# Running a graph's input stage beside the preceding graph's list stage in a graph-network kernel

## The chip, the cores and the metric

The kernel runs on one core of a Trainium2 chip. The metric is the device time of one execution in microseconds (us). Before the change three executions took 4073.46, 4090.68 and 4098.83 us; the median, 4090.68 us, is the number that the change is compared with. One further execution was profiled (4057.96 us, a profiled span of 4056.2 us); all lines of profile below come from it.

The engines have these names here: PE is the matrix engine (PEld its weight loads), DVE the vector engine, ACT the scalar engine, POOL the GpSimd engine, SP the engine that only issues DMA transfers. Each engine runs its own list of instructions in the order in which the program gives them, and waits at one that is not ready.

## The reference, cut to what matters

There are 16 graphs of 1024 nodes with 64 channels, and a weighted adjacency matrix per graph.

```python
x = _layernorm(x + _L0_gnn_ref(...))     # layer 0: messages = adj @ h; dh = tanh([h, messages] @ W1 + b1) @ W2 + b2
x = _layernorm(x + _L1_gnn_ref(...))     # layer 1, below

def _L1_gnn_ref(x, adj, mask, W1, b1, W2, b2):
    adj_d = _dilate_adj(adj, mask)                         # drops up to two neighbours of a node, by rank
    agg = _weighted_nanquantile_agg(x, adj_d > 0)          # per node and channel: sort the neighbours' values,
                                                           # weighted sum of the 0.25, 0.5, 0.75 quantiles
    out = x + agg
    return (relu(out @ W1 + b1) @ W2 + b2) * mask
```

The expensive part is that every node needs the values of its own neighbours sorted, channel by channel. Most nodes have few neighbours, a few (hubs) have very many.

## The kernel before

The kernel has two halves. The **front** of a graph reads its adjacency matrix, computes layer 0, orders the nodes by degree and makes each node's list of neighbours. The **units** gather the neighbours' rows from a table in HBM (one indirect DMA, issued by POOL, for each place of a list and each 128 nodes) and sort them on DVE with a network of min and max operations. Graphs are handled in groups of four: the units of a group start when its four fronts are there. The hubs of all graphs come last; the largest ones (168 neighbours) are one long DVE sort at the end.

```python
FRONT_NS, UNITS_NS = 185e3, 360e3      # estimated DVE time of a group's fronts, and of its units
...
def bank(name):                        # PSUM: 4 single banks, and two double ones (bank2)
    return psum.tile([P, HALF], F32, tag="bank", name=name, bufs=4)
...
desc = cp.tile([P, NT, N], F16, name="s_desc")     # N - column, for each of the 8 row tiles, 0 on the diagonal
...
def front(pool, grp, b, infs, out_ids, made):      # pool has one buffer of each tag unless it says more
    x_sb = pool.tile([P, NT, C], F32, tag="x_sb", name="x_sb", bufs=2)
    SY.dma_start(x_sb, x[b].rearrange("(t p) c -> p t c", p=P))
    score = pool.tile([P, NT, N], F16, tag="score", name="score")
    node = pool.tile([P, N], F32, tag="node", name="node")
    m = counts[:, b, :NT]
    for h in range(2):                             # ---- input stage: 8 row tiles
        pn = bank("pn")
        for k in range(NT // 2):
            t = h * (NT // 2) + k
            a_sb = pool.tile([P, N], F32, tag="a_sb", name="a_sb", bufs=3)
            SY.dma_start(a_sb, adj[b, t * P:(t + 1) * P, :])
            V.scalar_tensor_tensor(score[:, t, :], a_sb, 0.0, desc[:, t, :], op0=ALU.is_gt, op1=ALU.mult)
            ... # PE transposes a_sb through two banks, ACT copies them to aT
            junk = pool.tile([P, N], BF16, tag="junk", name="junk", bufs=2)
            A.activation(junk, score[:, t, :], AF.Sign, accum_out=m[:, t:t + 1])   # degree
            ... # PE: pn += x_sb and aT (messages)
            yield
        A.copy(node[:, h * HALF:(h + 1) * HALF], pn)
    ...                                            # ---- list stage: PE writes the keys of all nodes
    for t in range(NT):                            # ACT: the place of every node in the order by degree
        junk = pool.tile([P, N], BF16, tag="junk", name="junk", bufs=2)
        A.activation(junk, keys, AF.Sign, bias=nkey[:, t:t + 1], accum_out=place[:, t:t + 1])
    yield
    V.tensor_tensor(pre, pd.rearrange("p (t c) -> p t c", c=C), x_sb, op=ALU.add)
    yield
    ... # DVE: perm (8 operations, a yield after every second); PE: pi, and ps = perm x score, 8 x 16 matmuls
    yield from layernorm(pool, pre, rows[:, :, :C])
    ...
    for s in range(1, NT):
        V.max(mine_l[:, 1:9], slots[s])            # the first eight neighbours; two slots need a second round
        if s + 2 < NT:
            permuted(s + 2)                        # next 16 matmuls into a double bank
        yield
    ... # the neighbours to drop; POOL writes them to the table (removes); index and own for the units
    made.append((index, own))
    yield

def finish(pool, xs, u, mask, out_index):          # end of a unit: PE pu, ACT uT, PE ph, ACT hid, PE py in one go
    ...
    for _ in range(4):
        yield
    ... # DVE: residual, layernorm; POOL writes the rows out
```

A generator gives its turn away at each `yield`. The loop that builds the program takes a step of the fronts or of the units by comparing the estimated DVE time spent in each:

```python
def fronts(pool):
    for gi in range(groups):
        ...
        for g in range(G):
            yield from front(pool, grp, gi * G + g, infs, out_ids, made)   # one graph after the other
        ready[gi] = (infs, out_ids, made)
        yield
...
with tc.manual_schedule(engines={E.DVE, E.Activation, E.PE, E.Pool}):      # program order; SP is ordered by the framework
    ...
            behind = spent_f[0] / FRONT_NS - 1 <= spent_u[0] / UNITS_NS
            if behind or metered(work, spent_u) is False:                  # False: the next group isn't ready
                if metered(ahead, spent_f) == "over":
                    break
```

Of the kernel before, what the change touches and what calls it, by code (L numbers as in the profile page):

```python
# [11 lines left out]
F32 = mybir.dt.float32  # L12
F16 = mybir.dt.float16
# [13 lines left out]
C = 64  # L27
# [176 lines left out]
FRONT_NS, UNITS_NS = 185e3, 360e3  # L204
LW = 18

# [18 lines left out]
def sparse(ctx, tc, x, adj, nodemask, w1a, b1a, w2a, b2a, w1b, b1b, w2b, b2b, consts, out,  # L225
# [10 lines left out]
    def bank(name):  # L236
        return psum.tile([P, HALF], F32, tag="bank", name=name, bufs=4)
# [17 lines left out]
    desc = cp.tile([P, NT, N], F16, name="s_desc")  # L255
    GP.iota(desc, pattern=[[0, NT], [-1, N]], base=N, channel_multiplier=0,
# [34 lines left out]
    with tc.tile_pool(name="s_init", bufs=1) as pool:  # L291
        sel_f = pool.tile([2 * NT, NT * P], F32, name="sel_f")
        SY.dma_start(sel_f, consts[0:2 * NT, slice(*_CONSTS["sel"])])
        V.tensor_copy(sel.rearrange("k t p -> k (t p)"), sel_f)
        off_diag = pool.tile([P, P], F16, name="off_diag")
        V.tensor_scalar(off_diag, ident, -1.0, 1.0, op0=ALU.mult, op1=ALU.add)
        for t in range(NT):
            here = slice(t * P, (t + 1) * P)
            V.tensor_tensor(desc[:, t, here], desc[:, t, here], off_diag, op=ALU.mult)
        mask_u8 = pool.tile([P, P], U8, name="mask_u8")  # L300
        SY.dma_start(mask_u8, nodemask.rearrange("b (t p) -> (b t) p", p=P))
        mask_f = pool.tile([P, P], F32, name="mask_f")
        V.tensor_copy(mask_f, mask_u8)
        pm = bank("pm")
        T.transpose(pm[:, :P], mask_f, ident)
        V.memset(info, 0.0)
        V.tensor_copy(info[:, :, :, 1], pm[:, :P].rearrange("p (b t) -> p b t", t=NT))
        for b in range(B):
            V.tensor_copy(info[:, b, :, 0], node_id)
            V.tensor_copy(counts[:, b, NT:], rev)  # L310
# [15 lines left out]
    hub_infos = [dram.tile([B * n, 8], F32, name=f"hub_infos{c}")  # L326
# [4 lines left out]
    def layernorm(pool, src, dst):  # L331

        K = src.shape[1]
        mean = pool.tile([P, K], F32, tag="ln_mean", name="ln_mean")
        V.tensor_reduce(mean, src, axis=AX.X, op=ALU.add)
        V.tensor_scalar(mean, mean, 1.0 / C, None, op0=ALU.mult)
        xm = pool.tile([P, K, C], F32, tag="ln_xm", name="ln_xm")
        V.tensor_tensor(xm, src, mean.unsqueeze(2).to_broadcast([P, K, C]), op=ALU.subtract)
        sq = pool.tile([P, K, C], F32, tag="ln_sq", name="ln_sq")
        A.activation(sq, xm, AF.Square)  # L340
        yield
        yield
        var = pool.tile([P, K], F32, tag="ln_var", name="ln_var")
        V.tensor_reduce(var, sq, axis=AX.X, op=ALU.add)
        V.tensor_scalar(var, var, 1.0 / C, EPS, op0=ALU.mult, op1=ALU.add)
        e = pool.tile([P, K], F32, tag="ln_e", name="ln_e")
        A.activation(e, var, AF.Sqrt)
        yield
        yield
        y = pool.tile([P, K], F32, tag="ln_y", name="ln_y")  # L350
        V.reciprocal(y, e)

        V.tensor_tensor(e, y, y, op=ALU.mult)
        V.tensor_tensor(e, e, var, op=ALU.mult)
        V.tensor_scalar(e, e, -0.5, 1.5, op0=ALU.mult, op1=ALU.add)
        V.tensor_tensor(y, y, e, op=ALU.mult)
        V.tensor_tensor(dst, xm, y.unsqueeze(2).to_broadcast([P, K, C]), op=ALU.mult)

    def front(pool, grp, b, infs, out_ids, made):

        g = b % G
        x_sb = pool.tile([P, NT, C], F32, tag="x_sb", name="x_sb", bufs=2)
        SY.dma_start(x_sb, x[b].rearrange("(t p) c -> p t c", p=P))
        score = pool.tile([P, NT, N], F16, tag="score", name="score")
        node = pool.tile([P, N], F32, tag="node", name="node")
        m = counts[:, b, :NT]
        for h in range(2):
            pn = bank("pn")  # L370
            for k in range(NT // 2):
                t = h * (NT // 2) + k
                a_sb = pool.tile([P, N], F32, tag="a_sb", name="a_sb", bufs=3)
                SY.dma_start(a_sb, adj[b, t * P:(t + 1) * P, :])
                V.scalar_tensor_tensor(score[:, t, :], a_sb, 0.0, desc[:, t, :],
                                       op0=ALU.is_gt, op1=ALU.mult)
                aT = pool.tile([P, NT, P], F32, tag="aT", name="aT", bufs=2)
                for hh in range(2):
                    pt = bank("pt")
                    for kk in range(NT // 2):  # L380
                        jt = hh * (NT // 2) + kk
                        T.transpose(pt[:, kk * P:(kk + 1) * P], a_sb[:, jt * P:(jt + 1) * P],  # L382
                                    ident)
                    A.copy(aT[:, hh * (NT // 2):(hh + 1) * (NT // 2), :]  # L384
                           .rearrange("p a b -> p (a b)"), pt)
                junk = pool.tile([P, N], BF16, tag="junk", name="junk", bufs=2)
                A.activation(junk, score[:, t, :], AF.Sign, accum_out=m[:, t:t + 1])  # L387
                cols = slice(k * P, (k + 1) * P)
                T.transpose(pn[:C, cols], x_sb[:, t, :], ident)
                for jt in range(NT):  # L390
                    T.matmul(pn[C:, cols], x_sb[:, jt, :], aT[:, jt, :],  # L391
                             start=(jt == 0), stop=(jt == NT - 1))
                yield
            A.copy(node[:, h * HALF:(h + 1) * HALF], pn)


# [10 lines left out]
        hid = pool.tile([C, N], F32, tag="hid", name="hid")  # L407
        for h in range(2):
            ph = bank("ph")
            T.matmul(ph[:C], w1a_sb, node[:, h * HALF:(h + 1) * HALF], start=True, stop=True)  # L410
            A.activation(hid[:, h * HALF:(h + 1) * HALF], ph[:C], AF.Tanh, bias=b1a_sb)
# [5 lines left out]
        place = pool.tile([P, NT], F32, tag="place", name="place", bufs=2)  # L417
        for t in range(NT):
            junk = pool.tile([P, N], BF16, tag="junk", name="junk", bufs=2)
            A.activation(junk, keys, AF.Sign, bias=nkey[:, t:t + 1],  # L420
                         accum_out=place[:, t:t + 1])
# [38 lines left out]
        V.memset(lists, 0.0)  # L460
        V.tensor_scalar(lists[:, :, 0], inf[:, 1:, 0], -1.0, float(N), op0=ALU.mult, op1=ALU.add)
# [50 lines left out]
        V.tensor_scalar(removes, gone, -1.0, float(N), op0=ALU.mult, op1=ALU.add)  # L512
# [15 lines left out]
        hinf = pool.tile([P, 8], F32, tag="hinf", name="hinf", bufs=2)  # L528
        V.memset(hinf[:, 6:7], float(b * ROWS + N))
        V.memset(hinf[:, 7:8], float(b * N))  # L530
        V.tensor_copy(hinf[:, 0:3], inf[:, 0, 0:3])
        V.tensor_copy(hinf[:, 3:4], own[:, 0:1])
        V.tensor_copy(hinf[:, 4:6], gone[:, 0, :])
        for c, (first_slot, n, _, _) in enumerate(CLASSES):
            SY.dma_start(hub_infos[c][b * n:(b + 1) * n, :], hinf[first_slot:first_slot + n, :])

        index = grp.tile([P, NT - 1, LW], I32, tag=f"index{g}", name="index", bufs=2)
        V.tensor_scalar(index, lists, -1.0, float(N + b * ROWS), op0=ALU.mult, op1=ALU.add)
# [91 lines left out]
    def finish(pool, xs, u, mask, out_index):  # L630
# [6 lines left out]
        A.copy(uT, pu[:C, :K * P])  # L637
        ph = bank("ph1")
        T.matmul(ph[:, :K * P], w1b_sb, uT, start=True, stop=True)  # L639
        hid = pool.tile([H1, K * P], F32, tag="hid1", name="hid1")  # L640
        A.activation(hid, ph[:, :K * P], AF.Relu, bias=b1b_sb)
        py = bank("py")
# [4 lines left out]
        for _ in range(4):  # L647
            yield
# [13 lines left out]
    def hub_lists(pool, c, tiles, src, xpool, xtag, xbufs):  # L662
# [3 lines left out]
        hinf = pool.tile([P, K, 8], F32, tag="uhinf", name="uhinf", bufs=4)  # L666
        out_index = pool.tile([P, K], I32, tag="hout", name="hout", bufs=4)
        X = xpool.tile([P, cap + 1, K, W], F32, tag=xtag, name="X", bufs=xbufs)
        for k, tl in enumerate(tiles):
# [11 lines left out]
            for q in range(2):  # L681
                V.scalar_tensor_tensor(ls, ls, hinf[:, k, 4 + q:5 + q], ls,
                                       op0=ALU.not_equal, op1=ALU.mult)
            ix = pool.tile([P, rounds * 8], I32, tag="hub_ix", name="hub_ix")
            V.tensor_scalar(ix, ls, -1.0, hinf[:, k, 6:7], op0=ALU.mult, op1=ALU.add)
            me = pool.tile([P, 1], I32, tag="hub_me", name="hub_me", bufs=2)
            V.scalar_tensor_tensor(me, hinf[:, k, 0:1], -float(N), hinf[:, k, 6:7],
                                   op0=ALU.add, op1=ALU.add)
            V.tensor_tensor(out_index[:, k:k + 1], hinf[:, k, 0:1], hinf[:, k, 7:8], op=ALU.add)
# [52 lines left out]

    def fronts(pool):
        for gi in range(groups):
            infs = grp.tile([P, G, NT, 4], F32, tag="infs", name="infs")
            out_ids = grp.tile([P, G, NT], I32, tag="out_ids", name="out_ids")
            made = []
            for g in range(G):
                yield from front(pool, grp, gi * G + g, infs, out_ids, made)
            ready[gi] = (infs, out_ids, made)  # L750
            yield
# [79 lines left out]
    with tc.manual_schedule(engines={E.DVE, E.Activation, E.PE, E.Pool}), ExitStack() as body:  # L831
# [532 lines left out]
```

## Time and profile before

| what | us |
|---|---|
| median of three executions | 4090.68 |
| profiled span | 4056.2 |
| first gather of group 0 issued | 385.23 |
| last front's `removes` written by POOL | 2605.0 |
| span after 3600 us, in which DVE is busy 445.48 us | 456 |
| one indirect gather on POOL, mean of 960 | 1.137 |
| DVE score of one row tile, mean of 128 | 1.223 |
| ACT pass over the keys, one row tile, mean of 128 | 1.110 |
| DVE MAX8 over 1024 columns, mean of 112 | 1.231 |

How to read it: a "busy" time is the sum of the instructions of one engine, so engines overlap. A row of a table by stretch gives, for a stretch of the span, each engine's busy time and its number of instructions. A line of waits says which instruction stood idle, for whom, how long in total and how often. The granted TensorE clock (PEclk) is given as a share of the full one.

### The profile page before, as it was taken

To read this page: it belongs to the slowest core of one execution; us is meant where nothing else is said; L and a number is where in the kernel's file an instruction comes from. 1 tells how busy PE (TensorE), PEld (TensorE's weight loads), DVE (VectorE), ACT (ScalarE), POOL (GpSimd) and SP (SyncE) were. 2 spreads that over 40 slices of the span, in tenths; PEclk is the share of its full clock that TensorE was granted. 3 is DMA by queue.
4 is the path that set the end of the run, shared out by engine and by line. 5 is a ranking of instruction groups with operands and counts; after the bars stand their busy time and mean duration, and the time that the engine had idled before them with its cause. 6 is when DMAs were issued, how large, how long until landed. Compare 5 with 4: busy or idle time off the path is not lost.

```text
span 4056.2 us, 24404 instructions
## 1 busy us (share of the span) xinstructions
PE 1306.4 (32%) x7331; PEld 816.2 (20%) x7331; DVE 2525.3 (62%) x5216; ACT 629.3 (16%) x1252; POOL 1922.4 (47%) x1723
## 2 busy tenths in 40 slices
PE   4875125555604265472044447500101000000000
PEld 3443112332403032341031325200000000000000
DVE  3453119685595096448646564694645993279999
ACT  3332021321303021330030214200000000000000
POOL 0001745565187646405776630287776877710000
PEclk9887566777756576686566778755555555555555
DMA  5112221221113121211121212111111111100000
GB/s 105 53 61 52 37 44 24 62 65 25 55 21 68 24 57 34 58 55 17 23 65 29 65 23 69 25 21 24 24 31 24 22 21 25 26 6 1 0 0 1
DMA packets 131197, 146.26 MB, mean 36 GB/s; under 512 B 83424, under 2 KB 83616, under 8 KB 131056
## 3 DMA queue, kind: packets, MB, share of 16 engines
q0 software_dynamic: 54912, 56.92, 9.6%
q1 hardware_dynamic: 63664, 84.45, 6.9%
q10 hardware_dynamic: 12480, 3.24, 0.8%
q8 instruction: 60, 0.98, 0.1%
q14 instruction: 81, 0.66, 0.1%
HBM read 128.42 MB, written 16.06 MB: 36 GB/s over the span
## 4 chain that ended last, share of the span: by engine, by line
DVE 38%; POOL 18%; PE 16%; issue 13%; another core or an unknown queue 8%; ACT 5%; DMA 1%; ACTq 1%; DVEq 0%; POOLq 0%
DVE Y L220 25%; POOL X L544 17%; PE ps L447 8%; PE pn L391 5%; ACT junk L420 3%; DVE hub_list L220 2%; DVE hub_sc L220 2%; PE pt L382 2%; DVE lists L220 1%; POOL out_dram L657 1%; ACT aT L384 1%; DVE perm L220 1%; DVE nb L220 1%; DVE cnt L220 1%
## 5 line engine op out<-in xcount | busy, mean ns | idle before, releaser
L544 POOL DMA_INDIRECT X<-table,index x960 | 1091.0, 1137 | 301.7 <-issue 286.9
L220 DVE TENSOR_TENSOR Y<-Y 128x128 f32<-128x128 f32 (+10 forms) x1528 | 907.9, 630 | 92.9 <-remote 40.7
L544 POOL DMA_INDIRECT X<-table,hub_ix x580 | 622.2, 1073 | 176.8 <-issue 174.4
L447 PE MATMUL ps<-score,perm 128*128 128x512 f16 x2048 | 530.2, 422 | 179.0 <-issue 92.1
L220 DVE TENSOR_TENSOR Y<-Y,Y 128x256 f32<-128x256 f32 (+7 forms) x898 | 425.1, 512 | 57.8 <-issue 18.6
L635 PE MATMUL pu<-s_ident,u 128*64 128x128 f32 x128 | 29.3, 350 | 1315.2 <-DVE u L220 1245.6
L391 PE MATMUL pn<-aT,x_sb 128*64 128x128 f32 x2048 | 295.3, 305 | 389.6 <-ACT aT L384 228.6
L518 POOL DMA_INDIRECT table<-removes,at_row x32 | 36.3, 1134 | 809.5 <-DVE own L220 778.1
L391 PEld LDWEIGHTS pn<-aT,x_sb 128*64 128x64 f32 x2048 | 259.3, 155 | 427.2 <-ACT aT L384 260.6
L447 PEld LDWEIGHTS <-perm 128*128 128x128 f16 x2048 | 214.9, 106 | 486.1 <-issue 243.2
L220 DVE SCALAR_TENSOR_TENSOR score<-a_sb,s_desc 128x1024 f16<-128x1024 f32 x128 | 154.9, 1223 | 251.1 <-DMA a_sb<-in_adj_dram 250.8
L635 PEld LDWEIGHTS pu<-s_ident,u 128*64 128x64 f32 x128 | 14.4, 132 | 1324.8 <-issue 756.6
L657 POOL DMA_INDIRECT out_dram<-y,out_ids x112 | 128.8, 1150 | 276.9 <-DVE y L220 164.0
L220 DVE MAX8 lists<-ps 128x8 f16<-128x1024 f32 x112 | 137.6, 1231 | 184.1 <-PE ps L447 138.1
L657 POOL DMA_INDIRECT out_dram<-y,hout x16 | 18.7, 1170 | 485.4 <-DVE y L220 481.4
L639 PE MATMUL ph<-uT,s_w1b 64*128 64x512 f32 (+2 forms) x88 | 61.6, 796 | 519.8 <-ACT uT L637 426.8
L384 ACT COPY aT<-pt 128x512 f32<-128x512 f32 x256 | 139.0, 587 | 441.0 <-PE pt L382 320.0
L585 ACT ACTIVATE near<-near 128x72 f32<-128x72 f32 (+9 forms) x44 | 12.1, 274 | 1068.4 <-DVE near L220 793.7
L387 ACT ACTIVATE junk<-score 128x1024 bf16<-128x1024 f16 x128 | 136.4, 1066 | 180.6 <-DVE score L220 143.8
L382 PE MATMUL pt<-s_ident,a_sb 128*128 128x128 f32 x1024 | 155.5, 301 | 15.1 <-DMA a_sb<-in_adj_dram 15.1
L220 DVE TENSOR_TENSOR pre<-pd,x_sb 128x512 f32<-128x512 f32 x16 | 11.1, 692 | 236.0 <-PE pd L415 104.7
L420 ACT ACTIVATE junk<-keys,nkey 128x1024 bf16<-128x1024 f32 x128 | 140.0, 1110 | 0.0
(138 smaller groups left out, 1944.8 us busy)
## 6 DMA issues: line engine op xcount, KB each, us to landing
a_sb<-in_adj_dram SPq DMA_DIRECT2D x128, 512.0 KB
X<-table,index POOLq DMA_INDIRECT x960
X<-table,hub_ix POOLq DMA_INDIRECT x580
table<-s_rows SPq DMA_DIRECT2D x16, 264.0 KB
x_sb<-in_x_dram SPq DMA_DIRECT2D x16, 256.0 KB
hub_sc<-hub_scores SPq DMA_DIRECT2D x16, 256.0 KB
table<-s_rows ACTq DMA_DIRECT2D x12, 264.0 KB
hub_scores<-hub SPq DMA_DIRECT2D x16, 128.0 KB
```

Source lines behind the costliest of these rows:

```text
L220: return op(out, *args, **kw)
L382: T.transpose(pt[:, kk * P:(kk + 1) * P], a_sb[:, jt * P:(jt + 1) * P], ident)
L384: A.copy(aT[:, hh * (NT // 2):(hh + 1) * (NT // 2), :] .rearrange("p a b -> p (a b)"), pt)
L387: A.activation(junk, score[:, t, :], AF.Sign, accum_out=m[:, t:t + 1])
L391: T.matmul(pn[C:, cols], x_sb[:, jt, :], aT[:, jt, :], start=(jt == 0), stop=(jt == NT - 1))
L420: A.activation(junk, keys, AF.Sign, bias=nkey[:, t:t + 1], accum_out=place[:, t:t + 1])
L447: T.matmul(ps[:, h * HALF:(h + 1) * HALF], perm[:, t, s * P:(s + 1) * P], score[:, t, h * HALF:(h + 1) * HALF], start=(t == 0), stop=(t == ...
L518: GP.indirect_dma_start(out=pairs, out_offset=bass.IndirectOffsetOnAxis(ap=at_row[:, s:s + 1], axis=0), in_=removes[:, s, :], in_offset=None)
L544: GP.indirect_dma_start(out=X[:, d, k, :], out_offset=None, in_=src, in_offset=bass.IndirectOffsetOnAxis(ap=index, axis=0))
L635: T.transpose(pu[:C, k * P:(k + 1) * P], u[:, k, :], ident)
L639: T.matmul(ph[:, :K * P], w1b_sb, uT, start=True, stop=True)
L657: GP.indirect_dma_start(out=next(outs).rearrange("b n c -> (b n) c"), out_offset=bass.IndirectOffsetOnAxis(ap=out_index[k], axis=0), in_=y ...
```

## The change: what it does and what it is for

The front is cut into two generators: `front_in`, the eight row tiles, and `front_out`, everything after them. `beside` steps `front_out` of graph b and `front_in` of graph b + 1 alternately (26 steps against 8), so that PE and ACT have the next graph's tiles to work on where the list stage waits. This needs a second score buffer; the room comes from `desc`, which was one row of 1024 columns for each of eight row tiles and becomes a single row of 1920 columns read at a shift. The shift changes the numbers that the lists hold, so the lists are turned back into node numbers with a per-slot offset (`top`). `pn` gets a PSUM bank of its own, and the rotating banks go from four to three. The loads are issued three tiles ahead of use, and SP now keeps the program's order as well. The end of a unit is spread over more turns. The pacing constant for the units goes from 360 to 345.

```diff
-FRONT_NS, UNITS_NS = 185e3, 360e3
+FRONT_NS, UNITS_NS = 185e3, 345e3
...
-        return psum.tile([P, HALF], F32, tag="bank", name=name, bufs=4)
+        return psum.tile([P, HALF], F32, tag="bank", name=name, bufs=3)
...
-    desc = cp.tile([P, NT, N], F16, name="s_desc")
+    desc = cp.tile([P, 2 * N - P], F16, name="s_desc")
...
-    def front(pool, grp, b, infs, out_ids, made):
+    def load(pool, b, t):
+        a_sb = pool.tile([P, N], F32, tag="a_sb", name="a_sb", bufs=3)
+        SY.dma_start(a_sb, adj[b, t * P:(t + 1) * P, :])
+        return a_sb
...
+    def prefetch(pool, n):
+        for i in range(len(tiles), min(n, B * NT)):
+            tiles[i] = load(pool, i // NT, i % NT)
+
+    def front_in(pool, b, made):
+        x_sb = inputs[b]
+        score = pool.tile([P, NT, N], F16, tag="score", name="score", bufs=2)
...
-            pn = bank("pn")
+            pn = psum.tile([P, HALF], F32, tag="pn", name="pn", bufs=1)
...
-                V.scalar_tensor_tensor(score[:, t, :], a_sb, 0.0, desc[:, t, :],
+                a_sb = tiles[b * NT + t]
+                V.scalar_tensor_tensor(score[:, t, :], a_sb, 0.0,
+                                       desc[:, N - P - t * P:2 * N - P - t * P],
                                        op0=ALU.is_gt, op1=ALU.mult)
...
+                prefetch(pool, b * NT + t + 4)
                 yield
+                junk = pool.tile([P, N], BF16, tag="junk", name="junk")
+                A.activation(junk, score[:, t, :], AF.Sign, accum_out=m[:, t:t + 1])
...
+    def front_out(pool, grp, b, infs, out_ids, x_sb, score, node, made):
...
+        for t in range(NT):
+            junk = pool.tile([P, N], BF16, tag="junk", name="junk")
+            A.activation(junk, keys, AF.Sign, bias=nkey[:, t:t + 1],
+                         accum_out=place[:, t:t + 1])
+            if t % 3 == 2:
+                yield
...
-        V.tensor_scalar(index, lists, -1.0, float(N + b * ROWS), op0=ALU.mult, op1=ALU.add)
+        where = pool.tile([P, NT - 1, LW - 1], F32, tag="where", name="where")
+        V.scalar_tensor_tensor(where, lists[:, :, 1:], -1.0,
+                               top[:, 1:].unsqueeze(2).to_broadcast([P, NT - 1, LW - 1]),
+                               op0=ALU.mult, op1=ALU.add)
+        V.tensor_scalar(index[:, :, 1:], where, float(N), float(b * ROWS), op0=ALU.min, op1=ALU.add)
+        V.tensor_scalar(index[:, :, 0], inf[:, 1:, 0], float(b * ROWS), None, op0=ALU.add)
...
     def fronts(pool):
-        for gi in range(groups):
...
-            for g in range(G):
-                yield from front(pool, grp, gi * G + g, infs, out_ids, made)
-            ready[gi] = (infs, out_ids, made)
-            yield
+        inputs[0] = load_x(pool, 0)
+        prefetch(pool, 3)
+        inputs[1] = load_x(pool, 1)
+        done = []
+        yield from front_in(pool, 0, done)
+        for b in range(B):
...
+            out_b = front_out(pool, grp, b, infs, out_ids, *done[b], made)
+            if b + 1 < B:
+                yield from beside(out_b, front_in(pool, b + 1, done), 26, 8)
+            else:
+                yield from out_b
+            if b % G == G - 1:
+                ready[b // G] = (infs, out_ids, made)
...
-    with tc.manual_schedule(engines={E.DVE, E.Activation, E.PE, E.Pool}), ExitStack() as body:
+    with tc.manual_schedule(engines={E.DVE, E.Activation, E.PE, E.Pool, E.SP}), ExitStack() as body:
```

## The prediction, made blind

> **What bounds the kernel now.** I read the page first: the busy shares, then the 40 slices of about 101 us, because a kernel with stages is never bound by its average.
>
> ```profile
> PE 1306.4 (32%) x7331; PEld 816.2 (20%) x7331; DVE 2525.3 (62%) x5216; ACT 629.3 (16%) x1252; POOL 1922.4 (47%) x1723
> ...
> DVE  3453119685595096448646564694645993279999
> POOL 0001745565187646405776630287776877710000
> ```
>
> No engine is full on average. POOL is near 0 in slices 1 to 4, 11, 18 and 25 to 26, at 7 to 8 from slice 27 on, and then DVE is alone. So I took busy time by stretches, cut at POOL's gaps (stretch, length, then busy PE, PEld, DVE, ACT, POOL with counts; granted clock, DMA share, GB/s).
>
> ```profile
> 167.70:251.20 83.50, 64.94 (x423) 42.13 (x423) 39.17 (x75) 32.98 (x59) 3.29 (x2) 0.87 0.20 64
> ...
> 385.00:1002.00 617.00, 248.23 (x1319) 153.20 (x1320) 320.44 (x631) 114.95 (x226) 365.70 (x339) 0.66 0.22 43
> ...
> 1002.00:1096.00 94.00, 68.24 (x443) 43.29 (x442) 47.45 (x89) 32.89 (x59) 2.75 (x2) 0.88 0.18 57
> 1708.00:1848.00 140.00, 107.25 (x657) 62.74 (x655) 64.73 (x120) 48.33 (x85) 2.12 (x2) 0.84 0.15 44
> 2420.00:2602.00 182.00, 136.63 (x876) 86.68 (x874) 87.73 (x170) 65.86 (x118) 4.96 (x4) 0.87 0.15 46
> ...
> 2580.00:3600.00 1020.00, 77.29 (x246) 46.04 (x243) 645.42 (x1379) 33.39 (x105) 741.46 (x665) 0.51 0.15 23
> ```
>
> Four regimes. (a) Fronts alone: until 385, and in three later stretches of 94 + 140 + 182 = 416 us where the units have run out and the next group is not ready; POOL does almost nothing. (b) Fronts and units mixed: 617 us here, 612 and 572 in the next two groups. (c) Gathers only, about 1000 us: 741 busy, and 665 gathers leave about 0.3 us of issue time each, so POOL is the bound. (d) The last sort, 456 us, DVE alone. The change touches (a) and (b). POOL's waits between 380 and 2610 confirm (a):
>
> ```profile
> POOL table L518 <- DVE own L220: 420.9, 7, 80.7
> POOL X L544 <- issue: 326.2, 912, 14.4
> POOL out_dram L657 <- DVE y L220: 164.0, 8, 76.0
> ```
>
> The 420.9 us are waits for the end of a front, up to 80.7 us each. How one front spends its time shows in the chain, in time order, and in DVE's waits from 84 to 335, three graphs:
>
> ```profile
> 158.62 8.75 ACT junk L420 x16
> 167.61 3.27 DVE perm L220 x8
> 172.60 29.21 PE ps L447 x128
> ```
>
> ```profile
> DVE lists L220 <- PE ps L447: 39.1, 15, 5.0
> DVE score L220 <- DMA a_sb<-in_adj_dram: 28.9, 12, 4.0
> DVE place L220 <- ACT junk L420: 23.9, 4, 6.0
> DVE nkey L220 <- ACT junk L387: 20.3, 3, 6.9
> ```
>
> The work changes hands: PE stands still while ACT counts places, ACT while PE permutes. One graph takes 83.5 us, in which PE, the busiest, works 64.9, DVE 39.2, ACT 33.0.
>
> One oddity matters for regime (b). Between 1343 and 1417 consecutive `ps` matmuls start 2.80 us apart; in the front alone 128 of them take 29.21 us, 0.23 us each:
>
> ```profile
> 1343.33 0.59 PE L447 MATMUL ps<-score,perm 128*128 128x512 f16 x1 [2.64 <-issue]
> 1346.13 0.59 PE L447 MATMUL ps<-score,perm 128*128 128x512 f16 x1 [2.21 <-issue]
> ```
>
> PE crawls there, as around 410 to 580 and briefly around 2110 to 2160 and 2300 to 2350, mostly while POOL gathers without a pause and DVE stands still behind a front operation. I can't tell the cause.
>
> **What the Trainium skill says.** "Advanced Engine Details and Errata", Sequencer and Instruction Queues: the sequencer takes one instruction after the other, and each waits for its semaphores. The trace agrees: POOL stands at `removes` for 80.7 us. So a wait of a front also holds back the units behind it, on every engine. "TensorE: Matmul & The Clock Gate", Part 1: a busy PE is granted the full clock, an idle one half. It agrees here: 0.87 in the front alone, 0.51 in regime (c); fuller front stretches should not lose clock. "SBUF — State Buffer", SBUF: two separate sides: a DVE operation that holds the port pair which GpSimd shares keeps GpSimd from writing descriptors. It fits the gathers' 943 ns minimum against a mean of 1137 ns; DVE and POOL can't both be pushed to 100%. No page bears on the crawl at 2.80 us.
>
> **The change part by part.**
>
> *Overlap in front-alone stretches.* `front_in` is about 8 x 3.3 = 26 us of PE (16 `pn` matmuls every 3.28 us in the time order at 47 to 71), `front_out` the rest, 83.5 - 27 = 56. Side by side, PE's 64.9 us become the bound. I add 4 us for what no interleaving fills (PE behind DVE's `perm`, double banks that MAX8 frees late): 69 us a graph, 14.5 saved. Start: the first tile's copies come at 43.6, the first input stage ends at 71, four periods of 69 give 347 instead of 385: **38 us**. The later stretches of 416 us are 416 / 83.5 = 5.0 graphs: 5.0 x 14.5 = **73 us**.
>
> *Pacing.* Units cost about 290 us of DVE a group (437.9 busy between 1100 and 1830, less 4 x 39 for fronts = 282; 297 in the next). The fronts therefore advance 290 / 360 = 0.81 of a group while one group's units run, which explains why the deficit grows (1.1, 1.7, 2.2 graphs). With 345 it is 0.84: 0.035 x 4 = 0.14 graph a group, 0.14 + 0.28 + 0.42 = 0.84 graph in all, 58 us at 69. These fronts must still run in the mixed stretches; I count half: **29 us**.
>
> *Mixed stretches.* In 380 to 2580 DVE's waits at front operations add up to about 790 us (`pre` 224, `score` 183, `ln_var` 138, `lists` 124, `nkey` 75, `place` 48). The five front-alone graphs own 45 each, 225; the crawls about 330. Some 235 remain. Overlap should take half, 118, and half of that again counts, since POOL with its 340 or so instructions of about 1.38 us (470 of some 600 us) takes over soon: **59 us**. The extra turns in `finish` are in this.
>
> *What it adds.* Per graph one `where` (like the old `index`, 221 ns), an index copy, `top` and a little more on DVE, about 0.4 us; 16 graphs: 6 us. The `desc` constant is smaller (its iota took 7.0 us on POOL, once, hidden). Single `junk`, `pn` and three banks: before, `pn` held one of the four banks through four tiles, so three rotated anyway. Nothing for (c) and (d).
>
> Sum: 38 + 73 + 29 + 59 - 6 = 193; 4090.7 - 193 = 3898, rounded to **3890**.
>
> **The rivals.** *PE's crawl grows.* The mixed stretches receive denser PE work just when gathers run without a pause. For it: DVE's waits of 64, 62, 101 and 61 us fall there. Against it: where the kernel mixes both between 600 and 1000, matmuls run at their pace. If each group gets another 60 to 100 us, the result is about 4100 to 4150. *SP in program order.* A load now can't pass a store that waits for DVE; SP already waited 344 us at `hub_scores`, 524 us at `hub_infos`. Three tiles of prefetch (each 3.3 us of PE) cover only 10 us. If every front loses 8 us to it, 13 x 8 = 100 of the gain goes: about 4000. *DVE or POOL does better than I allow.* If the whole 235 us and the whole pacing gain come through and the next front's head start shortens the stretch before every group, another 150 to 200 us are there: about 3700. A stricter floor from POOL alone is far off: some 1700 indirect DMAs at 1.4 us after 347, and the last 456, give 3180.
>
> **Range and chances.** The 111 us of overlap in front-alone stretches are the safest part, 2.7%; the rest is worth between -100 and +250. Hence 3730 to 4040. Under 4008.9, the edge of 2%: 0.80; within 2%: 0.13; slower: 0.07.
>
> **What would show it.** Right: the first gather of group 0 near 347 instead of 385; a front-alone graph near 69 us with PE about 0.93 busy; POOL's waits for `own` falling from 421 to about 270; `place`, `nkey` and `pre` waits of DVE gone or small in those stretches; the stretch from the last front to the end still about 1450 us. Wrong: a graph's period still near 80 (then the three banks, the one `pn` or the two double banks bind it); long waits of DVE `score` for `a_sb` with SP standing at a store (the fixed order); more than about 330 us of DVE waits at `pn`- or `ps`-fed operations inside unbroken gathers (the crawl). If the time falls by far more than 200 us, my halving in the mixed stretches was the step at fault.

## The result and the profile after

The changed kernel took 3907.28 us (median of four executions, 3866.74 to 3946.60) beside 4090.38 us for the kernel before (four executions): a ratio of 0.948, 95% interval 0.942 to 0.955. Medians here are of all executions and ratios only of those within 1.5% of the kernel's fastest, so a ratio can differ from the quotient of the medians (here 0.955). The prediction said 3890. The total was close; the sum behind it holds only in part, and this section and the experiments show where.

The busy lines of the page and the two slice lines of the changed kernel (slices of 97 us), to lay beside those of before:

```profile
PE 1300.6 (34%) x7331; PEld 833.0 (22%) x7331; DVE 2524.6 (65%) x5281; ACT 638.9 (17%) x1252; POOL 1944.0 (50%) x1723
...
DVE  2554228874696763459667435975549972299999
POOL 0001757663187874408777710777767877700000
```

The work is the same: DVE is busy 2524.6 us against 2525.3, with 65 instructions more. The time came out of waits. POOL still falls to 0 or 1 in three places between its first and last slices.

The view by stretches of the changed kernel (stretch, length, busy PE, PEld, DVE, ACT, POOL with counts; granted clock, DMA share, GB/s). The first row is one period of the fronts at the start. The others are cut at the end of a group's last front (`own` written) and at the last gather before it, so mixed and front-alone stretches alternate:

```profile
150.00:228.00 78.00, 66.83 (x441) 44.73 (x440) 39.50 (x79) 34.84 (x61) 1.92 (x2) 0.89 0.22 65
371.00:904.00 533.00, 210.47 (x1126) 135.78 (x1126) 298.73 (x602) 100.08 (x198) 369.21 (x336) 0.63 0.22 45
904.00:1036.00 132.00, 109.62 (x665) 67.60 (x664) 73.00 (x143) 49.78 (x90) 8.74 (x8) 0.89 0.21 61
1036.00:1591.00 555.00, 209.60 (x1051) 132.69 (x1052) 387.82 (x829) 106.20 (x216) 397.61 (x342) 0.63 0.21 43
1591.00:1731.00 140.00, 120.32 (x775) 78.02 (x775) 66.71 (x132) 51.40 (x92) 8.25 (x10) 0.88 0.22 65
1731.00:2235.00 504.00, 164.23 (x842) 103.82 (x842) 350.07 (x744) 80.76 (x169) 394.11 (x341) 0.61 0.21 42
2235.00:2418.00 183.00, 131.45 (x781) 78.49 (x781) 94.80 (x198) 59.35 (x104) 11.44 (x10) 0.82 0.11 31
```

Cut in the same way (the prediction's cuts were coarser and gave 416 us for the front-alone part), the two kernels compare so, in us:

| | start, to the end of group 0's fronts | mixed stretches | front-alone stretches | after the last front | span |
|---|---|---|---|---|---|
| before | 378 | 615 + 596 + 555 = 1766 | 105 + 158 + 196 = 459 | 1454 | 4056 |
| after | 369 | 535 + 555 + 505 = 1595 | 132 + 140 + 183 = 455 | 1446 | 3865 |
| difference | -9 | **-171** | -4 | -8 | -191 |

The mixed stretches, for which the prediction allowed 59 us, bring 171 in this cut. The start and the front-alone stretches, which it called the safest part (111 us), bring 13.

How much falls to which stretch depends on the cut, because POOL and DVE do not leave a group's units at the same time. In the first and the third group POOL's last gather comes 14 us after DVE's last operation for the units before the change, and 12 and 31 us ahead of it after the change. A second cut goes by DVE: from the end of its last operation for a group's units to the `own` that completes the next group, DVE does fronts only (before 979 to 1098, 1671 to 1852 and 2393 to 2603; after 916 to 1036, 1569 to 1731 and 2267 to 2419). The sums of these three stretches, before and after, length first:

```profile
sum 510.00, PE 369.19 PEld 227.32 DVE 234.40 ACT 163.05 POOL 65.22; mean PE 123.06 PEld 75.77 DVE 78.13 ACT 54.35 POOL 21.74
sum 434.00, PE 350.69 PEld 223.53 DVE 228.20 ACT 166.12 POOL 36.77; mean PE 116.89 PEld 74.51 DVE 76.07 ACT 55.37 POOL 12.26
```

Cut so, the stretches of fronts alone bring 77 us and the mixed ones 98 (1714 to 1616). Both cuts give 175 for the two together.

POOL's waits in the changed kernel from 380 to 2430 go with the first cut: the wait for the fronts, 420.9 us before, is only a tenth shorter, and the one for the units' `y` is less than half of its 164.0:

```profile
POOL table L546 <- DVE own L221: 377.3, 7, 72.4
POOL X L578 <- issue: 311.6, 906, 19.0
POOL out_dram L692 <- DVE y L221: 72.7, 4, 30.3
```

*Why a front alone still takes 77 us.* PE's two waits while the changed kernel runs fronts alone (80 to 370):

```profile
PE pn L404 <- ACT aT L399: 21.0, 4, 6.0
PE ph L421 <- ACT node L410: 19.1, 4, 4.8
```

Each occurs once per graph, about 10 us together. The time order shows one of the second kind (start, duration, engine, line, operation; in brackets the idle time before it and its releaser):

```profile
207.83 2.29 DVE L221 TENSOR_TENSOR_SCAN cnt<-nb 128x1024 f16<-128x1024 f16 x1
...
212.69 1.22 DVE L221 SCALAR_TENSOR_TENSOR score<-a_sb,s_desc 128x1024 f16<-128x1024 f32 x1
214.01 1.06 ACT L409 ACTIVATE junk<-score 128x1024 bf16<-128x1024 f16 x1 [5.12 <-DVE score L221]
...
215.06 0.57 ACT L410 COPY node<-pn 128x512 f32<-128x512 f32 x1
...
215.68 1.12 PE L421 MATMUL ph<-node,s_w1a 128*64 128x512 f32 x1 [4.79 <-ACT node L410]
```

The `score` of the next graph's tile stands on DVE behind the end of this graph's list stage; ACT's degree pass waits for the score, the copy `node` stands behind the degree pass on ACT, and PE waits for `node`. The first kind is alike: ACT runs the eight place passes in one go, 144.98 to 154.85, and the copy `aT` that PE needs stands behind them. PE's work is there, but the queues of ACT and DVE hold back its inputs.

### The profile page after: what moved, and what is told of

Its sections match the earlier page's. It is cut to its first block, busy times and chain, and to the rows that moved or that the text cites. A ratio compares the mean times of both kernels' runs of the same rounds, so it can differ in the third digit from the quotient of the medians.

```text
span 3865.0 us, 24365 instructions
## 1 busy us (share of the span) xinstructions
PE 1300.6 (34%) x7331; PEld 833.0 (22%) x7331; DVE 2524.6 (65%) x5281; ACT 638.9 (17%) x1252; POOL 1944.0 (50%) x1723
## 5 line engine op out<-in xcount | busy, mean ns | idle before, releaser
L578 POOL DMA_INDIRECT X<-table,index x960 | 1120.7, 1167 | 301.3 <-issue 285.6
L578 POOL DMA_INDIRECT X<-table,hub_ix x580 | 610.1, 1052 | 176.8 <-issue 174.7
L472 PE MATMUL ps<-score,perm 128*128 128x512 f16 x2048 | 498.2, 403 | 64.8 <-DVE rest L221 27.1
L404 PE MATMUL pn<-aT,x_sb 128*64 128x128 f32 x2048 | 318.4, 320 | 317.3 <-issue 188.3
L404 PEld LDWEIGHTS pn<-aT,x_sb 128*64 128x64 f32 x2048 | 280.8, 164 | 358.6 <-issue 195.2
L472 PEld LDWEIGHTS <-perm 128*128 128x128 f16 x2048 | 204.8, 103 | 337.4 <-issue 105.7
L221 DVE MAX8 lists<-ps 128x8 f16<-128x1024 f32 x112 | 137.6, 1231 | 128.9 <-PE ps L472 128.4
L221 DVE SCALAR_TENSOR_TENSOR score<-a_sb,s_desc 128x1024 f16<-128x1024 f32 x128 | 154.9, 1216 | 36.4 <-DMA a_sb<-in_adj_dram 36.4
L221 DVE TENSOR_TENSOR pre<-py,infs 128x256 f32<-128x256 f32 (+1 forms) x32 | 12.5, 390 | 250.4 <-PE py L681 236.0
L674 PEld LDWEIGHTS ph<-uT,s_w1b 64*128 64x128 f32 x88 | 21.1, 296 | 710.3 <-ACT uT L671 437.1
L397 PE MATMUL pt<-s_ident,a_sb 128*128 128x128 f32 x1024 | 165.5, 314 | 6.9 <-DMA a_sb<-in_adj_dram 6.0
```

The lines of the kernel that those rows point to most:

```text
L221: return op(out, *args, **kw)
L404: T.matmul(pn[C:, cols], x_sb[:, jt, :], aT[:, jt, :], start=(jt == 0), stop=(jt == NT - 1))
L472: T.matmul(ps[:, h * HALF:(h + 1) * HALF], perm[:, t, s * P:(s + 1) * P], score[:, t, h * HALF:(h + 1) * HALF], start=(t == 0), stop=(t == ...
L578: GP.indirect_dma_start(out=X[:, d, k, :], out_offset=None, in_=src, in_offset=bass.IndirectOffsetOnAxis(ap=index, axis=0))
```

## The experiments

The theories. **O**: the gain is the overlap of the two stages, the same wherever the kernel runs. **L**: the gain is the load queue in the fixed order. **F**: the gain is the end of a unit spread over more turns. **C**: much of it is tied to PE's crawl (the prediction's oddity: PE far below its pace, mostly beside unbroken gathers), whose cost the new order keeps off DVE. **T**: the period of a front is set by where the input stage's steps lie between those of the list stage.

There were three sets of runs. On the chips of the first and the third, here A and C, no crawl was seen and the kernel before took 3668.86 and 3680.19 us; on the chip of the second, B, it took 4043.69, with the crawl. So A and C separate the change from the crawl, and B shows both together. Each ratio is to the kernel before on the same chip.

**Set 1, chip A: one part undone each time.** The expectations of this set are in times of the first measurement; since A takes 3669 us for the kernel before, only ratios can be compared. The changed kernel itself was not run on A; on C, in set 3, its ratio is 0.985. Sequential: the list stage first, then the next input stage; all else as changed.

```diff
-                yield from beside(out_b, front_in(pool, b + 1, done), 26, 8)
+                yield from out_b
+                yield from front_in(pool, b + 1, done)
```

> The changed kernel with the two generators one after the other again (front_out of b, then front_in of b + 1); everything else of the change stays. Theory O (the overlap carries the gain, mostly in the mixed stretches): nearly all of the 183 us comes back, 4040 to 4090, a front alone takes about 84 us, POOL's three mixed stretches return from 530, 560 and 505 to about 600. Theory L (loads ahead in SP's fixed order carry it, since DVE's score waits for a_sb went from 251 to 36 us): most of the gain stays, 3930 to 3980.

Measured: 3664.39 us, ratio 0.9989 (0.9976 to 1.0002). Without the overlap nothing is left.

The load queue left to the framework:

```diff
-    with tc.manual_schedule(engines={E.DVE, E.Activation, E.PE, E.Pool, E.SP}), ExitStack() as body:
+    with tc.manual_schedule(engines={E.DVE, E.Activation, E.PE, E.Pool}), ExitStack() as body:
```

> The changed kernel with SP's order left to the framework. Theory L: DVE's score waits for a_sb come back to 150 us or more and the time rises to 3980 to 4050. Theory O: within 30 us of the changed kernel, 3880 to 3940.

Measured: 3610.10 us, 0.9842 (0.9823 to 0.9861), the ratio of the changed kernel on C. L falls on this chip.

The old pacing constant:

```diff
-FRONT_NS, UNITS_NS = 185e3, 345e3
+FRONT_NS, UNITS_NS = 185e3, 360e3
```

> The changed kernel with UNITS_NS at 360 as before. By the prediction's pacing step it loses about 29 us: 3920 to 3950, with stretches of fronts alone longer by some 0.8 graph in all (60 us). The rival, that pacing hardly matters because what the fronts gain the units lose: within 10 us of the changed kernel.

Measured: 3668.01 us, 0.9991 (0.9978 to 1.0005). Overlap without the new constant brings nothing either.

The end of a unit in one go (the three yields between `uT`, `hid`, `py` taken out, four turns after `py`):

```diff
         A.copy(uT, pu[:C, :K * P])
-        yield
...
-        yield
+        for _ in range(4):
+            yield
```

> The changed kernel with the end of a unit in one go and four turns after it, as before. Theory F (the spread end of a unit carries much, since POOL's waits for y fell from 164 to 73 us in the groups): 3970 to 4010 and POOL's waits for y back to about 150 us. Theories O and L: 3890 to 3930; it might even gain, as DVE now waits 231 us at pre for PE py, which comes one turn after it.

Measured: 3606.05 us, 0.9823 (0.9804 to 0.9842). F falls on this chip.

**Set 2, chip B, with the crawl.** The changed kernel and the kernel before, each once more beside the same reference runs:

> The changed kernel unaltered, beside the kernel before on one chip. The first four experiments ran on a chip where the kernel before takes 3669 us instead of 4090. Theory C (PE's crawl at 2.80 us a matmul is a matter of the chip, and the larger part of the 183 us is crawl that the change steps around): where before is near 3670, the changed kernel is at 3600 to 3625, ratio 0.981 to 0.988; where before is near 4090, at about 3910. Theory O: the ratio is about 0.95 on any chip, 3480 where before takes 3670.

> The kernel before, for its trace. Theory C: if it takes about 3670 us here, no matmuls 2.8 us apart are found, the first gather of group 0 is still near 385 us, a front alone still takes 83 to 84 us, the last 456 us are unchanged, and the missing 420 us all lie between 385 and 2600. Rival: DMA or POOL is faster on this chip; then gathers take less than 1.25 us from start to start.

Measured: 3913.57 us, 0.966 (0.957 to 0.975), for the changed kernel, and 4013.85 us in one execution with a profile for the kernel before. Both have the crawl, and the change is worth 130 us here. The kernel before was thus not profiled without the crawl.

The input stage earlier beside the list stage:

```diff
-                yield from beside(out_b, front_in(pool, b + 1, done), 26, 8)
+                yield from beside(out_b, front_in(pool, b + 1, done), 18, 8)
```

> The changed kernel with the eight input tiles spread over the first 18 of the 26 list steps instead of all 26. Theory T (a front alone takes 78 us and not 69 since the last tile's score stands behind the list tail on DVE, and the node copy, ph and keys of the next graph wait for it): PE's wait of 4.8 us for ACT's node copy goes, a front alone takes 72 to 74 us, the first gather comes at about 355 instead of 376, and the time falls by 30 to 60 us against the changed kernel. Rival (PE is bound by its own half clock and the double banks): the period stays at 77 to 78 and the time within 10 us.

Measured: 3984.73 us, 0.985 (0.982 to 0.989), slower than the changed kernel. The first gather comes at 389.7 us, against 375.4 in the changed kernel; from one front's end to the next it takes 78 us at the start, against 77. T falls in this form: moving the steps trades one wait for another. PE's wait for `node` is gone, as expected, but the one for `aT`, 21.0 us over four graphs in the changed kernel, grew (90 to 380):

```profile
PE pn L404 <- ACT aT L399: 35.8, 7, 11.4
```

In the mixed stretches this run loses 117 us to the changed kernel on the same chip (1708 against 1591).

More DVE time for the fronts:

```diff
-FRONT_NS, UNITS_NS = 185e3, 345e3
+FRONT_NS, UNITS_NS = 185e3, 310e3
```

> The changed kernel with UNITS_NS at 310 instead of 345, so that the fronts advance 11% faster against the units. Between 360 and 345 lie about 60 us on the second chip (3668 against some 3607). Theory P (each front moved out of the stretches of fronts alone saves most of its 78 us there): 3540 to 3580 where before takes 3670. Rival (from 345 on the gathers of the group wait instead, nothing more to gain): 3595 to 3640.

Measured: 3879.67 us, 0.964 (0.954 to 0.974): not told apart from the changed kernel. (The times expected were those of a chip without the crawl.) Yet the inside changed completely: front-alone 232 us instead of 451 in the changed kernel on this chip, mixed 1813 instead of 1591.

**Set 3, chip C, without the crawl.** The changed kernel itself:

> The changed kernel itself, beside the others of this set. Theory C (what the change is worth depends on PE's crawl, because part of the gain is that crawling matmuls are moved out of the wait of DVE): on a chip without the crawl, where the kernel before takes about 3670 us, it takes about 3610, ratio 0.983; on a chip with the crawl (before about 4050 to 4090) 0.95 to 0.966, 3870 to 3920. Theory O (the gain is the overlap of the stages alone, the same on every chip): 0.95 on either, so 3490 where the kernel before takes 3670.

Measured: 3623.72 us, 0.985 (0.983 to 0.987). The size that C expected is confirmed and O refuted: the same change is worth 56 us here, 130 us on B and 183 us where it was predicted. How the crawl enters is not shown by this; the traces below bear on it.

The sequential kernel again:

> The list stage of a graph first, then the input stage of the next, everything else as in the changed kernel. Theory O: the time of the kernel before, ratio 0.99 to 1.01, on either kind of chip. Theory C on a chip with the crawl: the larger share of units (345) and the prefetched loads still take 30 to 60 us, but the crawl stays in DVE's wait: 0.985 to 1.0. Rival P (on a crawling chip prefetch and pacing carry the gain): 0.955 to 0.97. POOL's waits for DVE's own should be some 40 us above those of the changed kernel on the same chip.

Measured: 3675.36 us, 0.9986 (0.9979 to 0.9994); POOL's waits for `own` are 34.6 us above those of the changed kernel (293.6 against 259.0 from 380 to the last front). What this kernel does on a crawling chip was not measured, since this set fell on a quiet one.

The free load queue again:

> The load queue ordered by the framework, as in the kernel before. Theory L (the fixed order carries the gain on a crawling chip): 0.985 to 1.0. Its rival, that the early loads come from the program (three tiles ahead) and not from the order: within 0.5% of the changed kernel on the same chip, DVE's waits of score for a_sb below 60 us.

Measured: 3623.09 us, 0.985 (0.983 to 0.987), the changed kernel's own time; DVE's `score` waits 40.2 us for `a_sb` against 40.0. L is settled for a quiet chip: the loads come early because the program asks three tiles ahead.

The larger share for the fronts again:

> UNITS_NS 310 in place of 345. If the front-alone stretches are still owed to pacing: 10 to 35 us less than the changed kernel on the same chip, POOL's waits for DVE's own 40 us or more below it. If the fronts just take DVE's time from the units: within 10 us, or slower.

Measured: 3494.74 us (3492.03 to 3496.71), 0.950 (0.948 to 0.952): 129 us under the changed kernel, far more than the 10 to 35 us expected. It is the best kernel of this study on a quiet chip; on B it equals the changed kernel.

**The profiles cut alike**, in us. Mixed and front-alone are cut at POOL's last gather. "DVE fronts only" is the second cut, and "graphs" is the work of the fronts that DVE does in it, counted by the tiles that only fronts write and divided by that of one graph. It is the same for one program on every chip, since the order of the instructions is fixed. (In the sequential kernel the next graph's input stage follows this `own`, before the units start, and is not in it.)

| kernel | crawl | mixed | front-alone | DVE fronts only | graphs | after the last front | span |
|---|---|---|---|---|---|---|---|
| before (first profile) | yes | 1766 | 459 | 511 | 5.95 | 1454 | 4056 |
| before (B) | yes | 1729 | 452 | 503 | 5.94 | 1453 | 4012 |
| changed (first profile) | yes | 1595 | 455 | 434 | 5.77 | 1446 | 3865 |
| changed (B) | yes | 1591 | 451 | 425 | 5.77 | 1517 | 3929 |
| input early (B) | yes | 1708 | 441 | 461 | 5.77 | 1467 | 3999 |
| units 310 (B) | yes | 1813 | 232 | 276 | 3.77 | 1445 | 3860 |
| sequential (A) | no | 1512 | 332 | 426 | 5.21 | 1440 | 3664 |
| sequential (C) | no | 1515 | 332 | 425 | 5.21 | 1442 | 3667 |
| units 360 (A) | no | 1499 | 360 | 482 | 6.55 | 1442 | 3670 |
| changed (C) | no | 1509 | 298 | 418 | 5.77 | 1443 | 3622 |
| units 310 (C) | no | 1526 | 151 | 266 | 3.78 | 1444 | 3492 |

The free load queue (A and C) and the old end of a unit (A) come out like the changed kernel on C: mixed 1496 to 1504, front-alone 299 to 305, 5.76 to 5.77 graphs.

Without the crawl the mixed stretches last about 1500 to 1530 us whatever is done. The first one of the changed kernel on C, in the columns of the view by stretches:

```profile
372.00:861.00 489.00, 246.76 (x1369) 158.18 (x1369) 330.56 (x664) 117.25 (x229) 379.83 (x337) 0.70 0.28 56
```

and the same one of units 310 on C:

```profile
371.00:859.00 488.00, 264.25 (x1432) 170.08 (x1432) 337.65 (x691) 130.26 (x249) 378.94 (x337) 0.70 0.29 58
```

POOL is busy 379.83 us with 337 instructions, and POOL's own waits on C say what each costs besides:

```profile
POOL X L578 <- issue: 277.6, 901, 3.2
POOL table L546 <- DVE own L221: 259.0, 5, 72.5
```

277.6 / 901 is 0.308 us of issue, 104 us for 337. With the busy time that makes 484 of 489 us. POOL is the bound of the mixed stretches there, and a front's step beside them is nearly free: units 310 puts 63 more matmuls and 17 us of PE work in without a longer stretch, and all three stretches grow from 1509 to 1526 us. What remains to win is the front-alone time, which pacing sets in graphs and overlap in us per graph. At 310 POOL's wait for the fronts is halved:

```profile
POOL table L546 <- DVE own L221: 119.2, 3, 51.1
```

With the crawl the same stretches hold fewer fronts and last longer: the changed kernel's first one has 1126 matmuls in 533 us, against 1369 in 489. ACT's waits show the difference as time with no releaser that the profile knows ("issue", "remote"), as in the wait of `aT` for PE's transposes. Before, from 380 to 2610:

```profile
ACT aT L384 <- remote: 101.3, 10, 55.8
```

The changed kernel where it was predicted, 380 to 2430:

```profile
ACT aT L399 <- remote: 161.3, 14, 42.2
```

The changed kernel on C, 380 to 2190, where no such line stands and `aT` waits for the transposes by name:

```profile
ACT aT L399 <- PE pt L397: 295.7, 71, 19.3
```

The sums of all "issue" and "remote" waits between 380 and 2600:

| kernel | PE | ACT | DVE |
|---|---|---|---|
| before (first profile) | 269 | 450 | 226 |
| before (B) | 304 | 350 | 230 |
| changed (first profile) | 243 | 393 | 63 |
| changed (B) | 313 | 464 | 146 |
| input early (B) | 289 | 494 | 376 |
| units 310 (B) | 416 | 585 | 369 |
| changed, sequential, units 310 (A, C) | 0 | 0 to 6 | 0 to 6 |

The crawl itself hardly became shorter: PE's own sum goes from 269 to 243, on B from 304 to 313. What fell is the time in which DVE stands with such a wait, from 226 to 63, on B from 230 to 146: the crawl stands less in DVE's way. These sums miss the waits that name a releaser which is itself held up by the crawl. Before, DVE's largest waits between 380 and 993 name a load, and the longest, 452 to 517, falls where PE starts only 21 matmuls, after standstills like this:

```profile
DVE score L220 <- DMA a_sb<-in_adj_dram: 134.6, 5, 64.3
```

```profile
502.42 1.97 PE L391 MATMUL pn<-aT,x_sb 128*64 128x128 f32 x8 [53.45 <-issue]
```

And in the changed kernel DVE's largest wait, 38.9 us on C, is again mostly of this kind:

```profile
DVE pre L221 <- PE py L681: 231.0, 13, 74.0
```

Taken without names: in the three mixed stretches DVE's idle time (length less busy) fell from 697 us (1763 less 1066) to 555 (1592 less 1037).

## Why the prediction was right, and where it was not

The total held (3907 against 3890, well inside the range), in part by luck: errors of opposite sign cancelled. Cut at POOL's last gather, the steps for the start and the front-alone stretches were about 100 us too large (111 written, 13 found, with whatever pacing gave there), the one for the mixed stretches 112 us too small. Cut by DVE the errors are smaller: 86 us (9 and 77, again with whatever pacing gave) found for the 111, and 98 for the 59.

- **Overlap at the start, 38 us: failed in size.** The first gather moved from 385.2 to 375.4 us, 10 us. The step that failed is "Side by side, PE's 64.9 us become the bound. I add 4 us for what no interleaving fills": the period is 77 us, not 69, 12 us above PE's work and not 4, because PE's inputs stand behind other work on ACT and DVE twice a graph, 10 us. Of the three causes named as possible (three banks, one `pn`, double banks) only the last shows in PE's waits, with 0.9 us a graph (`ps` for ACT's copy `hub`). The wait chain is read from the time order; the one attempt to break it (the input stage earlier) did not shorten the period.
- **Overlap in later front-alone stretches, 73 us: about right where DVE does fronts only.** There 5.95 graphs took 511 us before and 5.77 take 434, 86 against 75 us a graph: some 11 us instead of 14.5, on more graphs than the 5.0 written, about 62 us. In the cut at POOL's last gather nothing is left of it (459 to 455), as the gathers now run out earlier against DVE. On C, between the sequential and the changed kernel, it is 9 us a graph (81.5 to 72.5).
- **Pacing, 29 us: mechanism and count right, but a cost left out.** From 360 to 345 the graphs fall from 6.55 to 5.77, and the step said 0.84. It is worth the full 58 us "at 69" and not half: on quiet chips 0.9991 against about 0.984. But the step overlooked a cost of nearly the same size in the change. A group is declared ready only after the input stage of the *next* graph is through, in the overlapped and in the sequential form: when group 0 is complete, DVE has run 40 `score` tiles in the changed kernel and 32 before. At the same 360 the overlapped kernel has 6.55 graphs left and the kernel before 5.95. So pacing (0.78) and this cost (0.60) nearly cancel, which fits that overlap at 360 and sequence at 345 each equal the kernel before. That the 0.60 come from the readiness test is read from the program and not tried apart, and the kernel before was not profiled on a quiet chip.
- **Mixed stretches, 59 us: right sign, too small.** They gave 171, or 98 in DVE's cut (62 on B, 1678 to 1616). The failing words are "the crawls about 330. Some 235 remain": the crawl was set aside as untouchable, and DVE's waits for it are what fell. On a quiet chip the step is worth about nothing at POOL's cut (1512 and 1515 sequential, 1509 changed), as POOL fills the stretch. The second half of the argument, "since POOL [...] takes over soon", is therefore what holds without the crawl.
- **What it adds, 6 us: not visible.** DVE's busy time is the same within 1 us.
- **Rival "PE's crawl grows": wrong for this change, right one step further.** At 345 the crawl's share of DVE fell. At 310 on B it ate the gain: front-alone -223 us, mixed +218 against the changed kernel; with the input stage earlier it took back about half of the gain (71 of 130 us).
- **Rival "SP in program order": wrong** on A and C, where it has no effect; with the crawl it was not tried.
- **"The last front to the end still about 1450 us": right**, 1446, and 1434 to 1467 in every other profile but one: the changed kernel on B took 1517, with POOL standing once for 73.2 us there. Why is open.

**What stays open.** Which part of the change keeps the crawl off DVE was not isolated, as the kernels with one part undone ran on quiet chips. That the order of the steps matters is shown (26 to 8 against 18 to 8, 0.966 against 0.985 on B), that the prefetched loads do is only suggested: DVE's `score` waits for `a_sb`, 182.7 us from 380 to 2610 before, of which 126 fall in the crawl at 452 to 581, sum to 36.4 in the whole changed run. And the cause of the crawl is unknown.

## What to carry to other kernels

When two streams share engines in program order, ask for each stretch which engine fills it: overlap inside a stretch that another engine bounds is free but worth nothing by itself, and only pays when the pacing hands the freed time to the stream that comes up short. Before calling one stretch the winner, cut the trace by a second engine: here 73 us changed sides between two cuts. Check the readiness test when stages are interleaved, as it may now wait for work of the next item. Re-tune the pacing constant after such a change (345 to 310 was worth more than the change itself where no crawl disturbed it), and try it on more than one chip.

## What was not expected of the hardware

The same kernel took 4044 to 4090 us in two sets and 3669 to 3680 in two others, 10% apart, and the three chips that were run longer, 23 to 31 executions each, kept to it (3996 to 4102 on B; 3649 to 3680 on A; 3671 to 3685 on C). The gathers do not differ: their minimum is 940 to 943 ns on all. DVE's operations do not either (MAX8 1231 and 1230 ns). The granted clock differs little, 0.63 to 0.65 as the span's mean.

What differs is PE between 380 and 2600. In the crawl of the changed kernel, by time order:

```profile
880.40 0.18 PE L461 MATMUL pi<-s_info,perm 128*128 128x4 f16 x1 [0.56 <-issue]
881.11 0.16 PE L461 MATMUL pi<-s_info,perm 128*128 128x4 f16 x1 [0.53 <-issue]
...
2189.35 0.27 PE L669 MATMUL pu<-s_ident,u 128*64 128x128 f32 x1 [1.43 <-issue]
2192.15 0.27 PE L669 MATMUL pu<-s_ident,u 128*64 128x128 f32 x1 [2.53 <-issue]
```

Matmuls of only four columns start 0.70 us apart, those of `pu` in f32 2.80 us apart, as `ps` of 512 columns did before. Many of the steps are multiples of 0.70 us, so it isn't the matmul's width alone. Most of the 243 us goes in longer standstills before `pn` (371 to 2430, up to 73.9 us at once):

```profile
PE pn L404 <- issue: 188.3, 17, 73.9
```

The Trainium skill's "TensorE: Matmul & The Clock Gate", Part 1, gives a full and a half rate for one busy core, 426.7 ns for 512 columns at half, and notes a quarter rate as an oddity; 2.80 us is 6.6 times the time at the half rate. The front-alone matmuls here come near the page's full rate (0.23 us beside its 215.7 ns), the crawl agrees with none of them, and the profile's granted clock hardly shows it: 0.63 in the first mixed stretch, 0.70 on C. The crawl came beside gathers, in every profile of B and of the first measurement, and in none of A and C. Whether it is a matter of the chip or of the occasion can't be told from this.
